# Seven block products for the query and output projections, and 2:4 comparisons summed in pairs

## The chip, the cores and the metric

The kernel runs on one core of one Trainium2 chip, in one launch. The metric is the device time in microseconds (us) of an execution, as the median over several runs; beside it stands one profiled execution, whose trace all views are read from. Engines are called as in the profile: PE (matrix multiplication), PEld (its weight loads), DVE (vector), ACT (scalar), POOL, and SP, whose queue issues all of the kernel's DMAs.

## The reference

Eight sequences of 512 tokens with 512 channels go through a "macaron" block, all in float32:

```
x = x + 0.5 * ffn(layernorm(x))        # FFN 1
x = x + attention(layernorm(x))        # 16 heads of 32 channels, 4 key/value heads
x = x + 0.5 * ffn(layernorm(x))        # FFN 2, same weights

ffn(x):        h = silu(x @ w_gate) * (x @ w_up)          # 2048 wide
               h = of each 4 neighbours keep the 2 largest in magnitude (ties: the first)
               return h @ w_down
attention(x):  Q = rope(x @ W_q); K = rope(x @ W_k); V = x @ W_v
               out = softmax(Q K^T / sqrt(32)) V           # K, V repeated over the heads
               return out @ W_o
```

`W_q` and `W_o` are 512 x 512; `W_k` and `W_v` are 512 x 128.

## The kernel before

**FFN.** There are 16 FFN passes (8 sequences, two each); each works through the hidden width in 4 pieces of 512 (`h`, indexed by `c`). The products of gate and up (`woven`, matmuls at L636) are not plain: each 512 x 512 product is cut into 2 x 2 blocks and made from seven block products instead of eight (a Strassen-Winograd scheme), with sums of blocks of the tokens (`ts`, made by `sums`) and sums of blocks of the weights (made once, in the first pass, by `combine_gu`, and kept in DRAM). The seven products go to three PSUM banks in the order x, v, x, v, x, z, x; between two products into a bank, DVE or ACT takes the bank's contents away (`copied`, L243 and L245, and `add`, L650), and the next product accumulates onto what is left in the bank. The down product (`products`, L561) is done the same way on blocks twice as deep; its weight sums are made by `combine_down` on POOL, its token-side sums `e` by POOL at L452 to L455.

**2:4 choice.** `keep_two_of_four` works on half of `h` at a time, [128, 4, 256]. ACT takes magnitudes (L407); DVE makes the six comparisons of the four neighbours as 0 or 1 in bf16 (L420 to L425), adds them up to four counts with eight operations on 128x256 elements (L429 to L441), and multiplies `h` by each count's comparison with a constant (L446). POOL's sums for the down product follow.

**Attention.** `attention(b)` runs as a "side": a generator whose steps are put between the products of the FFN passes of other sequences, so that PE always has FFN work between two steps. After its layernorm and transposes, `projected` makes K and then Q in four column blocks of 128, each with four matmuls 128x512 (L809) into one of three shared banks (`mm`); DVE rotates each block with four operations (shuffle of the bank, cosine times bank, sine times shuffle, add). V follows (L834). Then come, for each of four head groups, scores (L853) with maxima by DVE, transposed scores (L886, L891) with exponentials by ACT, the weighted sums (L902) and the division (L918 and after). Scores use a PSUM tile of four banks, `sc`. The output projection is four row blocks of 128 tokens with four matmuls 128x512 each (L988), and DVE adds each bank to the residual `xt` (L995), which goes to DRAM.

**What sets the order.** All instruction queues are written out in advance by a planner in the kernel: `at` holds its estimate of where PE, DVE and ACT stand; `multiplied` and `takes` advance it. DVE work that nobody needs at once is put in the queues `urgent` (`soon`), `put_off` (`later`) or `for_later`, and `fill`, called after each product, runs as much of it as is estimated to end with PE's queued work. `ensure` runs such work at once. A side has a first and a last place among the FFN products and a weight for each step (`WEIGHTS`); its next step is taken when it is due and its `ready` lies behind PE's place, or at the latest 3 groups (`LATE`) after it was due. One group is 3.45 us of PE time, as in L561's products of 16 records. PE, DVE, ACT, POOL and SP each run their own queue in order and meet through semaphores. Weight quarters of the FFN are prefetched 16 deep (`load_quarters`); `W_q`, `W_k`, `W_v` lie in one buffer of `wa_slots`, which `W_o` takes over.

Of the kernel before, what the change touches and what calls it, by code (L numbers as in the profile page):

```python
# [26 lines left out]
def macaron_block(  # L27
# [31 lines left out]
    wap = ctx.enter_context(tc.tile_pool(name="wap", bufs=1))  # L59
    qkvp = ctx.enter_context(tc.tile_pool(name="qkvp", bufs=1))  # L60
# [73 lines left out]
    identb = const.tile([P, P], BF, name="identb")  # L134

# [83 lines left out]
    wa_slots = Slots(wap, "wa", 1)  # L219
# [59 lines left out]
    def layernorm_t(got, tag, src=None, xb=None):  # L279
# [3 lines left out]
        xn = []  # L283
        for t in range(NT):
            xn.append(xnp.tile([P, D], FP, tag=tag, name="xn"))
            if xb is None:
                nc.sync.dma_start(out=xn[t], in_=src[t * P : (t + 1) * P, :])
# [39 lines left out]
        def sums():  # L327

            xT = got["xT"]
            (b11, b12), (b21, b22) = ([xT[:, 2 * i : 2 * i + 2, j * HALF : (j + 1) * HALF] for j in range(2)] for i in range(2))  # L330
            got["sums"] = ts = tp.tile([P, 4, 2, HALF], FP, tag="ts", name="ts")
            got["made"] = [
                later(0.62, partial(nc.vector.tensor_tensor, ts[:, i], a, b, ALU.subtract), at["act"])
                for i, a, b in ((0, b12, b11), (1, b22, ts[:, 0]), (2, b22, b12), (3, b21, ts[:, 1]))
            ]

        if xb is None:
# [21 lines left out]
            if tag == "xf":  # L359
                sums()  # L360
# [38 lines left out]
    def keep_two_of_four(h, made, sums=None, halves=(0, 1)):  # L399
# [14 lines left out]
        for half in halves:  # L414
            hh = h[:, :, half * HALF : (half + 1) * HALF]
            yield 0.7, at["act"] + HEARD

            m = sp.tile([P, 8, HALF], BF, tag="m", name="m")
            g01, g23, g02, g13, g03, g12, s0, s1 = (m[:, i, :] for i in range(8))
            nc.vector.tensor_tensor(m[:, 0:2, :], a[:, 0:4:2, :], a[:, 1:4:2, :], ALU.is_ge)  # L420
            yield 0.72, 0.0
            nc.vector.tensor_tensor(m[:, 2:4, :], a[:, 0:2, :], a[:, 2:4, :], ALU.is_ge)
            yield 0.7, 0.0
            nc.vector.tensor_tensor(g03, a[:, 0, :], a[:, 3, :], ALU.is_ge)
            nc.vector.tensor_tensor(g12, a[:, 1, :], a[:, 2, :], ALU.is_ge)  # L425
            taken = at["dve"]

            yield 0.4, 0.0
            nc.vector.tensor_tensor(s0, g01, g02, ALU.add)  # L429
            nc.vector.tensor_tensor(s1, g12, g13, ALU.add)  # L430
            yield 0.4, 0.0
            nc.vector.tensor_tensor(s0, s0, g03, ALU.add)
            nc.vector.tensor_tensor(s1, s1, g01, ALU.subtract)
            if half != halves[-1]:
                a = magnitudes(half + 1, taken + TOLD)
            yield 0.4, 0.0
            nc.vector.tensor_tensor(g02, g02, g12, ALU.add)
            nc.vector.tensor_tensor(g03, g03, g13, ALU.add)
            yield 0.4, 0.0
            nc.vector.tensor_tensor(g02, g23, g02, ALU.subtract)  # L440
            nc.vector.tensor_tensor(g03, g03, g23, ALU.add)  # L441
            for r, (s, op, n) in enumerate(
                ((s0, ALU.is_ge, 2.0), (s1, ALU.is_ge, 1.0), (g02, ALU.is_ge, 0.0), (g03, ALU.is_le, 1.0))
            ):
                yield 0.36, 0.0
                nc.vector.scalar_tensor_tensor(hh[:, r, :], s, n, hh[:, r, :], op, ALU.mult)  # L446
            if sums is not None:


                (h11, h21), (_, h22) = ([h[:, i::2, :HALF], h[:, i::2, HALF:]] for i in range(2))  # L450
                if half == 1:
                    nc.gpsimd.tensor_tensor(sums[:, 0], h21, h22, ALU.add)  # L452
                    nc.gpsimd.tensor_tensor(sums[:, 1], sums[:, 0], h11, ALU.subtract)
                    nc.gpsimd.tensor_tensor(sums[:, 2], h[:, 1::2, :HALF], sums[:, 1], ALU.subtract)
                    nc.gpsimd.tensor_tensor(h21, h11, h21, ALU.subtract)  # L455
            thin["halves"] = half + 1
# [39 lines left out]
    def combine_down(g):  # L496

        for c in range(2 * g, 2 * g + 2):
            raw = p_slots.tile([P, 4, D], FP, "raw")
            for r in range(4):  # L500
                nc.sync.dma_start(out=raw[:, r], in_=w_down[c][:, r])
                there = at["pe"] + 5.0
                yield now if r < 3 else lambda: there
            quarter = {f"{i + 1}{j + 1}": raw[:, i::2, j * HD2 : (j + 1) * HD2] for i in range(2) for j in range(2)}
            sums = wa_slots.tile([P, 6, 2, HD2], FP, "sums")

            for i, name in enumerate(SUMS):
                of = quarter[name[3:]] if name[3:] in quarter else sums[:, int(name[4:]) - 1]
                nc.gpsimd.tensor_tensor(sums[:, i], quarter[name[:2]], of, ALU.subtract)
                nc.sync.dma_start(out=combined[g, name][:, c % 2 * 2 : c % 2 * 2 + 2, :], in_=sums[:, i])  # L510
            yield now
# [270 lines left out]

    def attention(b):
        ensure(written[b, 0])
        wa = wa_slots.tile([P, ND, D + 2 * KV], FP, "wqkv")
        cs = p_slots.tile([P, 4, S], FP, "cs")
        loads = deque()
        for src, col in ((w_k, D), (w_v, D + KV)):
            loads.append((wa[:, :, col : col + KV], src.rearrange("(c p) n -> p c n", p=P)))
        for i in range(2):  # L790
            loads.append((cs[:, i], rope[i]))
        for k in range(ND):
            loads.append((wa[:, k, :D], w_q[k * P : (k + 1) * P, :]))
        got = {}
        for ready in layernorm_t(got, "xa", tokens[b][1]):
            if loads:
                dst, src = loads.popleft()
                nc.sync.dma_start(out=dst, in_=src)
# [6 lines left out]
        def projected(dst, col, scale):  # L805

            ps = Bank([P, S], "proj")
            for k in range(ND):
                nc.tensor.matmul(  # L809
                    out=ps.tile, lhsT=wa[:, k, col : col + P], rhs=xT[:, k, :], start=(k == 0), stop=(k == ND - 1)  # L810
                )
            multiplied(3.43)
            fill()
            sw = w_slots.tile([P, S], FP, "sw")
            soon(0.65, partial(nc.vector.stream_shuffle, sw, ps.tile, SWAP))
            read = soon(
                0.62, partial(nc.vector.scalar_tensor_tensor, dst, ps.tile, scale, cs[:, 0, :], ALU.mult, ALU.mult)
            )
            ps.free([read])
            soon(0.65, partial(nc.vector.scalar_tensor_tensor, sw, sw, scale, cs[:, 1, :], ALU.mult, ALU.mult))  # L820
            made = soon(0.65, partial(nc.vector.tensor_tensor, dst, dst, sw, ALU.add))
            return [p_slots.used(w_slots.used(made), 1)]

        of_k = projected(kT, D, 1.0)
        yield now
        of_q = []
        for c in range(ND):
            of_q.append(projected(qT[:, c, :], c * P, 1.0 / math.sqrt(HD)))
            yield now
        ensure(of_q[-1])  # L830
        vps = Bank([P, NT, KV], "vps")
        for t in range(NT):
            for k in range(ND):
# [3 lines left out]
                    rhs=wa[:, k, D + KV : D + 2 * KV],  # L837
# [7 lines left out]
        wo = wa_slots.tile([P, ND, D + 2 * KV], FP, "wo")  # L845
        yield partial(when, of_k + of_q[0])
# [88 lines left out]
        ensure(of_k + of_q[0])  # L935
        for t in range(NT):
            found = scores(0, t, nm)
            nc.sync.dma_start(out=wo[:, t, :D], in_=w_o[t * P : (t + 1) * P, :])
# [40 lines left out]
        xts = []  # L979
        for t in range(NT):  # L980
            xts.append(xnp.tile([P, D], FP, tag="xa", name="xt"))
            nc.sync.dma_start(out=xts[t], in_=tokens[b][1][t * P : (t + 1) * P, :])
        yield partial(when, out_of)
        waits(ensure(out_of))
        for t, xt in enumerate(xts):
            y = Bank([P, D], "y")
            for k in range(ND):
                nc.tensor.matmul(  # L988
                    out=y.tile, lhsT=qT[:, k, t * P : (t + 1) * P], rhs=wo[:, k, :D], start=(k == 0), stop=(k == ND - 1)
                )  # L990
            multiplied(3.43)
            fill()

            def add(t=t, xt=xt, y=y):
                nc.vector.tensor_tensor(xt, y.tile, xt, ALU.add)  # L995
                nc.sync.dma_start(out=tokens[b][2][t * P : (t + 1) * P, :], in_=xt)

            made = [soon(0.62, add)]
            y.free(made)
            if t == NT - 1:  # L1000
                ensure(made)
            yield now
# [8 lines left out]
    WEIGHTS = [0.5] * (NORM + ND + 2) + [0.7] * (NT + 1) + [0.9, 0.9] * NT  # L1011
    WEIGHTS += ([0.9, 1.2] + [0.9, 0.9] * (NT - 1)) * (ND - 2) + [1.5] + [1.3] * (NT - 1) + [1.5] + [0.5] * NT
# [6 lines left out]
    sides = [(10, 19, 10, partial(combine_down, 0), None, None), (22, 34, 10, partial(combine_down, 1), None, None)]  # L1019
# [109 lines left out]
```

## Time and profile before

| | us |
|---|---|
| median of 3 runs | 3211.94 |
| lowest, highest | 3211.62, 3216.32 |
| profiled execution, its own time | 3210.11 |
| its span, first to last instruction | 3208.2 |
| PE busy in it | 3176.9 |
| PEld busy | 2322.4 |
| DVE busy | 2189.8 |
| ACT busy | 1195.8 |
| POOL busy | 507.2 |

How to read it: the span is what the views cover; the profiled execution adds 1.9 us around it. A float32 matmul appears as two PE records. Records of neighbouring instructions overlap, since they are pipelined: what an instruction costs its engine is the distance from its start to the next one's start, which the chain and the timeline show, and not the record's own length. Idle time of an engine counts only if PE, whose work is nearly the whole span, ends up waiting for it.

### The profile page before, as it was taken

Reading aid. Unit: us, or ns where it says so; the run is one execution under the profiler, and the core shown is the slowest. Engines: PE = TensorE matmul, PEld = TensorE weight load, DVE = VectorE, ACT = ScalarE, POOL = GpSimd, SP = SyncE. Lnnn points to the kernel's source line nnn. Section 1 sums busy time; section 2 is a strip of 40 time slices with the busy share of each in tenths; the row PEclk is TensorE's granted clock in tenths of the full one; section 3 lists DMA queues with packets and bytes.
Section 4 is the critical chain, followed back from the end, with each engine's and each line's share of the span. In section 5 each row is a group of like instructions: output and inputs, shape, how many; then the busy total and the mean of one; then the engine's idle time right before and its main releaser. Section 6 shows DMA issues by size and latency. Waiting matters only on the chain.

```text
span 3208.2 us, 43276 instructions
## 1 busy us (share of the span) xinstructions
PE 3176.9 (99%) x15880; PEld 2322.4 (72%) x15880; DVE 2189.8 (68%) x4718; ACT 1195.8 (37%) x1683; POOL 507.2 (16%) x822
## 2 busy tenths in 40 slices
PE   8999999999999999999999999999999999999999
PEld 6887767767677677766776677766776677666886
DVE  7756876587657785678657865777567765776554
ACT  2222454145522553245314542255324441454220
POOL 2322102110021111101211102111120121111110
PEclk9999999999999999999999999999999999999999
DMA  7763344434443436334444344443633444434441
GB/s 236 240 216 99 122 158 144 142 128 126 156 158 126 132 119 210 96 121 152 145 143 131 122 153 159 133 132 112 210 99 119 161 141 142 131 122 154 154 165 53
DMA packets 263731, 462.15 MB, mean 144 GB/s; under 512 B 25952, under 2 KB 81760, under 8 KB 263264
## 3 DMA queue, kind: packets, MB, share of 16 engines
q1 hardware_dynamic: 263520, 459.38, 44.2%
q8 instruction: 127, 2.08, 0.3%
q14 instruction: 84, 0.69, 0.1%
HBM read 421.53 MB, written 37.75 MB: 143 GB/s over the span
## 4 chain that ended last, share of the span: by engine, by line
PE 96%; DVE 2%; DMA 1%; ACT 1%; POOL 0%; issue 0%; SPq 0%; POOLq 0%; DVEq 0%
PE x L636 27%; PE v L636 13%; PE x L561 13%; PE z L636 7%; PE v L561 6%; PE proj L809 4%; PE st L886 4%; PE sc L853 4%; PE ops L902 4%; PE y L988 3%; PE z L561 3%; PE tr L263 1%; PE gu L611 1%; PE den L918 1%; PE vps L834 1%; PE st L891 1%
## 5 line engine op out<-in xcount | busy, mean ns | idle before, releaser
L636 PE MATMUL x<-ts,w 128*128 128x256 f32 x3000 | 717.3, 382 | 1.4 <-DVE corner L650 1.4
L636 PEld LDWEIGHTS x<-ts,w 128*128 128x128 f32 x3000 | 561.7, 190 | 137.9 <-issue 44.3
L452 POOL TENSOR_TENSOR e<-h 128x512 f32<-128x512 f32 x62 | 79.3, 1279 | 2232.5 <-DVE h L446 1892.9
L165 DVE TENSOR_REDUCE nm<-sc 128x1 f32<-128x512 f32 x512 | 321.1, 683 | 95.3 <-PE sc L853 94.0
L561 PE MATMUL x<-wd,h 128*128 128x256 f32 x1488 | 339.9, 382 | 0.0
L165 DVE TENSOR_TENSOR total<-total,p 128x512 f32<-128x512 f32 x384 | 273.8, 749 | 81.1 <-ACT p L894 81.1
L561 PEld LDWEIGHTS x<-wd,h 128*128 128x128 f32 x1488 | 280.2, 190 | 62.5 <-issue 19.3
L894 ACT ACTIVATE p<-st 128x2048 f32<-128x2048 f32 x96 | 179.7, 1872 | 291.1 <-PE st L891 279.8
L255 ACT ACT_TABLE_LOAD x215 | 275.8, 1283 | 4.5 <-PEq L1118 0.7
L243 ACT COPY row<-x 128x512 f32<-128x512 f32 x207 | 121.2, 585 | 393.0 <-PE x L636 392.9
L685 ACT ACTIVATE h<-x 128x256 f32<-128x256 f32 x125 | 47.6, 381 | 555.2 <-PE x L636 543.3
L636 PE MATMUL v<-ts,w 128*128 128x256 f32 x1000 | 239.0, 382 | 2.4 <-ACT xT L324 2.4
L636 PE MATMUL x<-xT,w 128*128 128x256 f32 x1000 | 239.4, 382 | 1.8 <-ACT xT L324 1.8
L636 PE MATMUL v<-xT,w 128*128 128x256 f32 x1000 | 238.5, 382 | 1.5 <-DVE corner L245 1.5
L636 PE MATMUL z<-xT,w 128*128 128x256 f32 x1000 | 238.9, 382 | 0.0
L561 PE MATMUL v<-wd,e 128*128 128x256 f32 x992 | 228.2, 382 | 7.1 <-POOL e L452 4.0
L561 PEld LDWEIGHTS v<-wd,e 128*128 128x128 f32 x992 | 186.2, 190 | 52.6 <-issue 13.3
L636 PEld LDWEIGHTS x<-xT,w 128*128 128x128 f32 x1000 | 186.9, 190 | 49.2 <-issue 20.4
L636 PEld LDWEIGHTS v<-ts,w 128*128 128x128 f32 x1000 | 187.3, 190 | 46.2 <-issue 16.2
L636 PEld LDWEIGHTS z<-xT,w 128*128 128x128 f32 x1000 | 187.1, 190 | 45.6 <-issue 19.3
L636 PEld LDWEIGHTS v<-xT,w 128*128 128x128 f32 x1000 | 187.7, 190 | 42.8 <-issue 10.1
L407 ACT ACTIVATE a<-h 128x1024 f32<-128x1024 f32 x128 | 134.9, 1054 | 186.0 <-DVE m L425 106.8
(115 smaller groups left out, 4448.8 us busy)
## 6 DMA issues: line engine op xcount, KB each, us to landing
w<-gu SPq DMA_DIRECT2D x472, 256.0 KB, 3.4
w<-in_w_gu SPq DMA_DIRECT2D x394, 256.0 KB, 3.4
wd<-wd SPq DMA_DIRECT2D x124, 512.0 KB, 5.4
wd<-in_w_down SPq DMA_DIRECT2D x186, 256.0 KB, 3.6
x<-x SPq DMA_DIRECT2D x64, 256.0 KB, 2.6
xn<-x SPq DMA_DIRECT2D x64, 256.0 KB, 5.0
x<-in_x SPq DMA_DIRECT2D x32, 256.0 KB, 3.7
gu<-w SPq DMA_DIRECT2D x32, 256.0 KB, 2.9
```

Of the source, the lines that this page charges most:

```text
L165: self.does()
L243: nc.scalar.copy(dst, src)
L255: nc.scalar.activation(dummy[:, 1:2], dummy[:, 0:1], f)
L407: nc.scalar.activation(a, h[:, :, half * HALF : (half + 1) * HALF], AF.Abs)
L561: nc.tensor.matmul(out=y.tile[:, t, :], lhsT=part[:, t * P : (t + 1) * P], rhs=operands[i][:, n, :], start=(first and t == 0 and n == 0), ...
L636: nc.tensor.matmul(out=bank.tile[:, m, :], lhsT=lhs[:, m, k, :], rhs=rhs[:, k, :], start=(first and m == 0 and k == 0), stop=(k == 1), ski ...
L809: nc.tensor.matmul(out=ps.tile, lhsT=wa[:, k, col : col + P], rhs=xT[:, k, :], start=(k == 0), stop=(k == ND - 1))
L853: nc.tensor.matmul(out=sc[:, kv, :], lhsT=qT[rows, c, t * P : (t + 1) * P], rhs=kT[rows, :], start=True, stop=True)
L886: nc.tensor.matmul(out=st[:, kv, :], lhsT=kT[rows, t * P : (t + 1) * P], rhs=qT[rows, c, :], start=True, stop=False)
L894: nc.scalar.activation(p, st, AF.Exp)
L902: nc.tensor.matmul(out=ops[rows, :], lhsT=v[:, t, rows], rhs=p[:, kv, :], start=(t == 0), stop=(t == NT - 1))
L988: nc.tensor.matmul(out=y.tile, lhsT=qT[:, k, t * P : (t + 1) * P], rhs=wo[:, k, :D], start=(k == 0), stop=(k == ND - 1))
```

## The change

1. Q (without K) and the output projection are each made by seven block products, as in `woven`: blocks of 256 x 256, each product four matmuls 128x256, in the first three banks of the score tile `sc`, in the bank order 0, 1, 0, 1, 0, 2, 0. A product into a bank that was used before waits until DVE or ACT has taken what the bank held.
2. The sums of blocks of `W_q` and `W_o` are made once, by DVE, in the second FFN pass, and kept in DRAM. Weights then come one block (256 KB) at a time into a pool `waq` of 4 buffers, each loaded as one is used up.
3. The attention's tokens get sums of blocks too (`sums`, four DVE operations), and so do the heads' outputs (`combined_heads`, four more). The partial results are copied or added into `qT`, or added to the residual in place.
4. Scores begin when all of Q is rotated, not its first block alone. The rotation works on blocks of [128, 2, 256].
5. The table of cosines and sines is loaded once, not in each attention.
6. `combine_down` writes its sums in the four buffers of `waq`, not in one tile of `wa_slots`. The residual and the attention's layernorm input are one tile of four rows each, not four tiles.
7. In the 2:4 choice, five operations take the place of eight for the counts: three on two counts at once (128x512), one of which reads one comparison twice by a broadcast, and two on 128x256.
8. Steps and weights of the side follow.

```
@@ keep_two_of_four
-            nc.vector.tensor_tensor(s0, g01, g02, ALU.add)
-            nc.vector.tensor_tensor(s1, g12, g13, ALU.add)
-            nc.vector.tensor_tensor(s0, s0, g03, ALU.add)
-            nc.vector.tensor_tensor(s1, s1, g01, ALU.subtract)
...
-            nc.vector.tensor_tensor(g02, g02, g12, ALU.add)
-            nc.vector.tensor_tensor(g03, g03, g13, ALU.add)
-            nc.vector.tensor_tensor(g02, g23, g02, ALU.subtract)
-            nc.vector.tensor_tensor(g03, g03, g23, ALU.add)
+            g12, g03 = m[:, 5, :], m[:, 4:5, :].to_broadcast([P, 2, HALF])
+            g01_02, g13_23, g01_23, g02_13 = m[:, 0:2, :], m[:, 2:4, :], m[:, 0:4:3, :], m[:, 1:3, :]
...
+            s0_3 = m[:, 6:8, :]
+            nc.vector.tensor_tensor(s0_3, g01_23, g02_13, ALU.add)
+            nc.vector.tensor_tensor(g13_23, g13_23, g01_02, ALU.subtract)
...
+            nc.vector.tensor_tensor(s0_3, s0_3, g03, ALU.add)
+            s1, s2 = m[:, 2, :], m[:, 3, :]
+            nc.vector.tensor_tensor(s1, s1, g12, ALU.add)
+            nc.vector.tensor_tensor(s2, s2, g12, ALU.subtract)

@@ new: weights
+    def combine_qo():
+        for which, how in (("q", Q_SUMS), ("o", O_SUMS)):
+            both = [p_slots.tile([P, 4, 2, HALF], FP, "both") for _ in range(2)]
+            w = [both[q // 4][:, q % 4] for q in range(8)]
+            for q in range(4):
+                nc.sync.dma_start(out=w[q].rearrange("p a b -> p (a b)"), in_=flat(qo_raw[which][q]))
...
+            for to, a, b, op in how:
+                made = later(0.65, partial(nc.vector.tensor_tensor, w[to], w[a], w[b], op), queue=for_later)
+            yield partial(when, [made])
+            ensure([made])
+            nc.sync.dma_start(out=qo_sums[which], in_=both[1])
+            yield now

@@ attention: in place of projected() for Q
+        def seven(lhs, rhs, take):
+            sc = sc_slots.tile([P, N_KV, 2, HALF], FP, "seven")
+            waits(sc_slots.ready)
+            order = 0, 1, 0, 1, 0, 2, 0
+            taken = {bank: [] for bank in order}
+            for i, bank in enumerate(order):
+                waits(ensure(taken[bank]))
+                w = weights.popleft()
+                for m in range(2):
+                    for k in range(2):
+                        nc.tensor.matmul(out=sc[:, bank, m, :], lhsT=lhs(w, i, m, k), rhs=rhs(w, i, k), ...)
+                multiplied(1.73)
+                load_next()
+                fill()
+                taken[bank] = take(i, sc[:, bank])
...
+                yield partial(when, taken[order[i + 1]] if i < 6 else [])
...
+        def take_query(i, bank):
...
+            if i < 3:
+                return [Done(copied((left, corner, right)[i], bank))]
+            if i == 6:
+                return rotate(below, 0, bank)
+            to, j = ((right, 1), (corner, 1), (left, 0))[i - 3]
+            entry = soon(0.62, partial(nc.vector.tensor_tensor, to, bank, to, ALU.add))
+            rotate(to, j)
+            return [entry]
...
-        ensure(of_k + of_q[0])
+        ensure(of_k + of_q)

@@ attention: in place of the four row blocks of the output
+        made = [soon(0.62, partial(nc.vector.tensor_tensor, combined_heads[:, i], a, b_, op)) ...]   # 4 sums
+        def take_output(i, bank):
+            def add(to):
+                nc.vector.tensor_tensor(to, bank, to, ALU.add)
+                if i >= 5:
+                    for t in (0, 1) if i == 5 else (2, 3):
+                        nc.sync.dma_start(out=tokens[b][2][t * P : (t + 1) * P, :], in_=xt[:, t, :])
...

@@ the sides
-    WEIGHTS = [0.5] * (NORM + ND + 2) + ...  + [1.5] + [0.5] * NT
+    WEIGHTS = [0.5] * (NORM + 2 + 7 + 1) + ... + [1.5, 0.7] + [0.5] * 7
+    sides gets (36, 40, 2, load_cs, ...), (43, 56, 12, combine_qo, ...)
```

## The prediction

> **What bounds the kernel now.** I read the page's head first, then the chain that ended last.
>
> ```profile
> span 3208.2 us, 43276 instructions
> PE 3176.9 (99%) x15880; PEld 2322.4 (72%) x15880; DVE 2189.8 (68%) x4718; ACT 1195.8 (37%) x1683; POOL 507.2 (16%) x822
> PEclk9999999999999999999999999999999999999999
> PE 96%; DVE 2%; DMA 1%; ACT 1%; POOL 0%; issue 0%; SPq 0%; POOLq 0%; DVEq 0%
> ```
>
> PE's work is the span, at the full granted clock. The waits of PE alone say how little it lacks:
>
> ```profile
> PE tr L263 <- DVE xn L373: 7.4, 3, 6.4
> PE v L561 <- POOL e L452: 4.0, 4, 1.5
> PE st L886 <- DVE nm L165: 3.1, 2, 1.5
> PE v L561 <- DMA wd<-in_w_down: 2.9, 1, 2.9
> ...
> PE v L636 <- DVE corner L245: 1.5, 1, 1.5
> ...
> PE x L636 <- DVE corner L650: 1.4, 2, 1.2
> ```
>
> All of PE's waits together are some 27 us, 7.4 of them in the opening. So what this change is worth is decided by how many PE microseconds it removes, and by whether it gives PE something new to wait for. The rows of the matmuls concerned, by shape:
>
> ```profile
> L636 PE MATMUL x<-ts,w 128*128 128x256 f32 x3000 | 717.3, 382 | 1.4 <-DVE corner L650 1.4
> L636 PEld LDWEIGHTS x<-ts,w 128*128 128x128 f32 x3000 | 561.7, 190 | 137.9 <-issue 44.3 <-ACT corner L243 6.1 <-DVE row L650 4.0
> L809 PE MATMUL proj<-xT,wqkv 128*128 128x512 f32 x320 | 143.8, 592 | 0.0
> L988 PE MATMUL y<-wo,qT 128*128 128x512 f32 x256 | 115.1, 592 | 0.0
> L432 DVE TENSOR_TENSOR m<-m 128x256 bf16<-128x256 bf16 x128 | 37.2, 291 | 0.0
> ```
>
> The durations 382 and 592 ns overlap; prices are taken from the chain in order of time (start, us, what), in the first attention's projections:
>
> ```profile
> 245.31 1.73 PE x L636 x8
> 247.03 1.73 PE z L636 x8
> 248.76 3.43 PE proj L809 x8
> 252.19 1.73 PE x L636 x8
> 253.92 3.43 PE proj L809 x8
> 257.35 3.45 PE x L561 x16
> ```
>
> A block product (4 matmuls 128x256, 8 records) costs 1.73 us; a projection of one column block (4 matmuls 128x512, 8 records) 3.43. Changing from one kind to the other costs nothing. Between two steps of the side lies 1.73 to 3.45 us of FFN work on PE.
>
> **The change, part by part.**
>
> *PE work.* Q takes 4 x 3.43 = 13.72 us per attention now and 7 x 1.73 = 12.11 after: 1.61 less. With the finer distances (429 ns for 128x512, 215.7 for 128x256: 32 x 0.429 = 13.73 against 56 x 0.2157 = 12.08) it is 1.65. The output projection is the same again. 16 projections in 8 attentions: between 25.8 and 26.4, taken as **-26.2 us**. K, V, scores and FFN keep their matmuls; transposes too.
>
> [...] These weights fill all rows, and seven products need 56 loads where four blocks need 32. [...]
>
> *Waits between products.* Each seven has four re-uses of a bank (products 3, 4, 5 and 7), 64 in all. Uncovered, each would cost about 0.9 us (a DVE add of a bank is 0.69, and some 0.1 each for hearing of PE and for PE hearing of it): 58 us. The nearest row is L636 itself, which runs the same order of banks 125 times, with one product between a take and the next use, and waits for `corner` 2.9 us in all: 2.9 x 16 / 125 = 0.4 us. The side's products have FFN work between them besides, and are put off until their `ready`. I take **+0.5**. What is new beside L636 is that a taken bank may stand behind a rotation in the urgent queue; that is a rival below.
>
> *Scores wait for all of Q.* The last block comes with product 7: shuffle, cosine, sine, add, 0.60 to 0.71 us apart in the timeline, about 2.6 us, before the first score. Once per attention, 8 x 2.6 = 21 us if nothing covers it; the step is held back until the planner sees it ready and FFN products of 1.73 us go in its place. I take 0, with that upper end. K is ready long before.
>
> *DVE.* Per attention: 4 token sums, 3 adds and up to 3 copies for Q (ACT takes some, 0.585 each), 4 sums of heads and 3 more adds for the output: 14 to 17 operations of 0.69, 9.7 to 11.7 us, 77 to 94 in eight; rotations are as many as before. Once, 8 weight sums of 0.78 (the row of `w<-w`, L705): 6 us. The counts of the 2:4 choice cost 8 x 0.20 = 1.61 us per half now (start to start in the timeline; the records of 283 overlap). No row has a 128x512 bf16 addition. Its bounds are 0.20 and 0.60 us, the distance at 256 bf16 and at 512 f32 elements. [...] None of it is on PE's path; what hides it is DVE's idle 32%. That cover is thinnest in the projections: in 240 to 283 us DVE is busy 31.7 of 43, and gets 5 to 7 more. At 85 to 90% it still fits; a queue there shows as PE waits for `row` or `corner`, which I put at **+1.5** for all eight. The shorter counts might take back part of the 4.0 us of waits for `e`: -0.5, at most -4.
>
> *DMA and SP's queue.* Per attention, 4 loads of `W_q`, 4 of `W_o` and 2 of cosines become 14 blocks of 256 KB: 4 issues more (0.34 us each on SP) and 1 MB more, 8 MB on 462. SP waits for PE most of the time already (731 us for L636 alone), with 16 quarters, some 28 us of PE work, loaded ahead; a block load waiting for its buffer holds those behind it no longer than one product. A block lands in some 5 us (`wqkv` now); four are ahead, so at least three products and the FFN work between, 12 us or more. 0. The loads of `xn` for the next attention wait for the last store of `xt` (3.5 us) as the fourth does now: 0. The weight sums add 4 MB in the second pass, where DMA moves 99 to 122 GB/s against 240 before it, and the sums are due 2 groups before the first attention: 0, or up to 6 if DVE is forced through them at once. Three shared `mm` banks are freed from Q and output; PE waits for none there now: 0. POOL's sums for the down weights get the same four buffers in turns: 0.
>
> *Order.* The sides' steps fall on other places among the products, so that chance meetings, such as PE waiting about 1 us for a transposed block (at six places now), come and go: 0, by about 3 either way.
>
> Sum: -26.2 + 0.5 + 1.5 - 0.5 = **-24.7**. The profiled execution took 3210.11 (span and 1.9 around it), which is 1.8 under the median of the runs. 3210.1 - 24.7 = 3185.4, and 1.8 on top is 3187.2 for the median, 0.77% less: I say **3187**.
>
> **The rivals.**
>
> *A. Half the gain is lost in Q's phase.* A taken bank stands in the urgent queue behind a rotation: product 7 needs the add of product 5, which is behind the rotation of block 4, 2.6 us, and its own 0.6. If the planner lets it come late, PE waits 1 to 2 us per attention, and an FFN add behind it as long: about 12 us. 3199. For it: DVE at 85 to 90% there. Against: the same four operations stand in DVE's queue in the projections now, and no PE wait comes of them.
>
> *B. The same queue becomes the bound: slower.* The place is the stretch from product 4 of Q to the first score. A step that is not ready is forced 3 groups after it was due. If DVE is behind by more than that, PE stands for the rest of the rotations: up to 3.2 for product 7, then 2.6 for the last rotation, and again on FFN banks. It decides from 26.2 / 8 = 3.3 us per attention; with 5 us each it is -26 + 40, 3226. Against: 3 groups are 10 us, and DVE's queue would have to fall that far behind, with 15% of its time free.
>
> [...]
>
> **How the numbers follow.** Forecast 0.68 (own range 3180 to 3196), C with PE covered 0.06 (3190), A 0.10 (3193 to 3208), B 0.12 (over 3212), and 0.04 for something small that cancels all. Below 3180 is possible if the order also removes waits: hence 3178 as the low end. The high end goes up to 3208, into A; what is left out is B and a little below. A measurement of this kernel can tell about 0.2%, 6.4 us: faster is below 3205.5. That holds the forecast, C and most of A: 0.81. Same 0.07: the rest of A and the small one. Slower 0.12: B.
>
> **What would show it right or wrong.** No row of PE with 128x512 but K's and the last FFN's; a new row of 896 records, for Q and output together, 382 ns, starting 216 apart; PE busy about 26 us less, span about 25 less. PE's waits by these products and by scores under 5 us together; over 25 us there is B. [...] I am wrong if weight loads show between the new records, if the FFN's rows get idle time before them from DVE, or if steps of the side are forced before DVE is done with the bank.

## The result, and the profile after

The changed kernel takes 3194.55 us (median of 6 runs, 3193.66 to 3198.68), the kernel before 3214.89 in the same session (6 runs): a ratio of 0.994, 95% interval 0.9927 to 0.9953, faster by some 20 us. The forecast was 3187 in 3178 to 3208, and faster. Beside later experiments the changed kernel took 3194.47 against 3211.76, ratio 0.9944 (0.9932 to 0.9957).

The head of the page after, and its chain by engine:

```profile
span 3192.6 us, 43897 instructions
PE 3152.0 (99%) x16264; PEld 2391.1 (75%) x16264; DVE 2256.3 (71%) x4458; ACT 1176.2 (37%) x1663; POOL 525.6 (16%) x822
PE 92%; DVE 4%; DMA 2%; POOL 1%; ACT 1%; issue 0%; SPq 0%; DVEq 0%; POOLq 0%; ACTq 0%
```

PE is busy 24.9 us less, DVE 66.5 more, weight loads 69 more, and PE's share of the chain is down from 96% to 92%: PE waits more often. The span is only 15.6 shorter. (The profiled execution of before, 3210.11, lies 4.8 under the median of its six runs, that of after 0.1 under its own; so the two traces show 16 us of the 20.)

The new products, in two of their four groups by shape, and three of the counts of the 2:4 choice:

```profile
L889 PE MATMUL seven<-waq,sums 128*128 128x256 f32 x256 | 60.5, 379 | 0.0
L889 PEld LDWEIGHTS seven<-waq,sums 128*128 128x128 f32 x256 | 48.6, 190 | 6.6
L908 PE MATMUL proj<-xT,wkv 128*128 128x512 f32 x64 | 28.8, 592 | 0.0
L439 DVE TENSOR_TENSOR m<-m 128x512 bf16<-128x512 bf16 x128 | 55.6, 434 | 0.0
L441 DVE TENSOR_TENSOR m<-m 128x512 bf16<-128x512 bf16 x128 | 55.2, 431 | 3.3
L445 DVE TENSOR_TENSOR m<-m 128x512 bf16<-128x512 bf16 x128 | 54.5, 426 | 0.0
```

No PE idle time before the 896 records of L889, and hardly any for their weight loads. 128x512 is left to K in the projections. From each record's start to the next one's, Q and output took 219.9 us before (a wait of 0.8 behind them left out) and L889 takes 193.4: 26.5 saved.

What PE waits for, longest first (in total, times, longest):

```profile
PE v L569 <- POOL e L460: 11.5, 8, 2.0
PE tr L264 <- DVE xn L381: 7.6, 3, 6.5
PE v L569 <- DMA wd<-in_w_down: 3.2, 1, 3.2
PE st L1002 <- DVE nm L167: 3.1, 4, 1.8
PE vps L919 <- DVE kT L167: 2.4, 3, 0.8
```

Nothing waits in `seven`. But waits for `e`, the down product's sums that POOL makes after the 2:4 choice, went from 4.0 to 11.5 us, and V waits for K's bank, 2.4. All PE waits: 27.5 before, 36.7 after. And the granted clock is no longer full throughout. In these views (stretch, length, busy us of PE, PEld, DVE, ACT, POOL, then the clock) the stretches are cut at the steps of 3.41 us by which the clock changed in these traces, as the last section shows. Before:

```profile
103.41:106.83 3.42, 2.11 (x10) 1.52 (x8) 3.42 (x8) 1.00 (x1) 0.51 (x1) 1.00 0.87 308
106.83:110.24 3.41, 1.77 (x8) 1.39 (x9) 3.38 (x12) 0.06 (x1) 0.00 (x0) 1.00 1.01 358
```

and after

```profile
104.61:108.03 3.42, 0.18 (x2) 0.17 (x2) 3.38 (x11) 1.06 (x1) 0.00 (x0) 1.00 1.02 364
108.03:111.44 3.41, 3.41 (x9) 2.70 (x10) 2.44 (x6) 0.00 (x0) 1.01 (x2) 0.50 1.05 368
```

After PE's 3.2 us wait for `wd` the clock is at half for 3.4 us, which costs 1.7: the 16 records of L569 behind the wait take 5.38 us, and 3.62 at full clock. Before, the same wait (2.9) had no such sequel: it fell across two of these stretches and left PE idle for 1.3 and 1.6 us of them, where the 3.2 us lie in one. The balance of the two traces: -26.5 in the projections, +9.2 of waits and +1.7 of clock make -15.6, as in the span.

### The profile page after: what moved, and what is told of

The parts are those of the page before. It is cut to its first block, busy times and chain, and to the rows that moved or that the text cites. A ratio compares the mean times of both kernels' runs of the same rounds, so it can differ in the third digit from the quotient of the medians.

```text
span 3192.6 us, 43897 instructions
## 1 busy us (share of the span) xinstructions
PE 3152.0 (99%) x16264; PEld 2391.1 (75%) x16264; DVE 2256.3 (71%) x4458; ACT 1176.2 (37%) x1663; POOL 525.6 (16%) x822
## 4 chain that ended last, share of the span: by engine, by line
PE 92%; DVE 4%; DMA 2%; POOL 1%; ACT 1%; issue 0%; SPq 0%; DVEq 0%; POOLq 0%; ACTq 0%
PE x L644 25%; PE v L644 13%; PE x L569 13%; PE v L569 7%; PE z L644 6%; PE seven L889 6%; PE st L1002 4%; PE sc L969 4%; PE ops L1018 4%; PE z L569 3%; PE tr L264 1%; PE gu L619 1%; PE vps L919 1%; PE den L1034 1%; PE st L1007 1%; PE y L602 1%
## 5 line engine op out<-in xcount | busy, mean ns | idle before, releaser
L569 PE MATMUL x<-wd,h 128*128 128x256 f32 x1488 | 340.1, 382 | 0.8 <-DVE x L583 0.8
L569 PEld LDWEIGHTS x<-wd,h 128*128 128x128 f32 x1488 | 279.4, 190 | 61.6 <-issue 14.2
L569 PE MATMUL v<-wd,e 128*128 128x256 f32 x992 | 230.3, 384 | 14.8 <-POOL e L460 11.5
L569 PEld LDWEIGHTS v<-wd,e 128*128 128x128 f32 x992 | 187.2, 191 | 57.5 <-POOL e L460 14.7
```

Of the source, the lines that this page charges most:

```text
L569: nc.tensor.matmul(out=y.tile[:, t, :], lhsT=part[:, t * P : (t + 1) * P], rhs=operands[i][:, n, :], start=(first and t == 0 and n == 0), ...
```

## The experiments

### Which part brings the time: the 2:4 counts alone, seven alone, Q alone

`two_four_alone` is the kernel before with the five operations; `seven_alone` the changed one with the eight.

> The kernel before with the five-operation counts of the 2:4 choice alone. By the prediction DVE is busy some 10 us less (1.53 us per half by the starts in the trace, against 1.62) and the time is within 3 us of before, since PE does not wait for it; e waits between 1 and 5 us. If the planner's too low cost (0.34 counted for an operation that starts its successor 0.45 later) makes DVE late, e waits rise by 3 to 6 us, and the time with them.

> The changed kernel with the old eight-operation counts of the 2:4 choice. If the choice is off PE's path, the time is that of the changed kernel within 3 us (20 under before), with DVE busier by about 10 us. If the shorter counts were what kept e early, e waits grow from 11.5 by 0.1 to 0.2 per half in the tight places, 2 to 4 us more.

Counts alone: 3214.21 us against 3212.23, ratio 1.0004 (0.9995 to 1.0013): nothing. DVE is busy 2171.3 instead of 2189.8 (18.5 less, where 10 were expected), and PE's waits for `e` are 4.2. Seven alone: 3198.12, ratio 0.9955 (0.9942 to 0.9967), DVE 2278.9, waits for `e` 13.5 and for `nm` 8.9. So the gain comes with the products; under them the shorter counts may be worth some 4 us, but the intervals of 0.9955 and 0.994 overlap.

In `q_only` the output keeps its four blocks, with `W_o` by rows in the buffers of `waq`:

```
-        coming_qo = deque([("q", q) for q in SEVEN_Q] + [("o", q) for q in SEVEN_O])
+        coming_qo = deque([("q", q) for q in SEVEN_Q] + [("row", k) for k in range(ND)])
...
+                nc.tensor.matmul(out=y.tile, lhsT=qT[:, k, t * P : (t + 1) * P], rhs=wo[k], ...)   # for k, for t
```

> The changed kernel with the old output projection (four blocks of four matmuls 128x512, W_o by rows in the four buffers of waq). PE's work is 13.1 us over the changed kernel's; if the gain is PE work, the time is 8 to 13 us under before, and the row of the products in seven is 96.7 us long where the changed kernel's was 193.4. Waits for e are set by places, 6 to 9 us.

3203.97 us, ratio 0.9973 (0.9963 to 0.9984), 8.4 under before's 3212.4: half the products, about half the gain. The seven's starts span 96.8 us. The output's row is back:

```profile
L1108 PE MATMUL y<-waq,qT 128*128 128x512 f32 x256 | 115.1, 592 | 0.0
L892 PE MATMUL seven<-ts,waq 128*128 128x256 f32 x256 | 60.6, 380 | 0.0
```

Its waits for `e` are 8.4.

### Why PE waits more for e: less room, or other places

The changed side has 4 more steps before the scores and 4 more at the end, in the same length. From the first score to the last division's matmuls an attention has 213 to 225 us in the trace after, 233 to 239 before. First idea: the softmax's DVE work is squeezed, and the 2:4 choice is late. `before_squeezed` squeezes the kernel before by weights alone:

```
-    WEIGHTS = [0.5] * (NORM + ND + 2) + ...  + [1.5] + [0.5] * NT
+    WEIGHTS = [0.61] * (NORM + ND + 2) + ... + [1.5] + [1.03] * NT
```

> The kernel before, with no arithmetic changed: only the side's weights for layernorm, projections and output are raised (0.5 to 0.61, and 0.5 to 1.03 in the output), so that the stretch from the first score to the last division has as little room as in the changed kernel (some 220 us an attention in place of 236). Theory 'squeeze' (the same DVE work of the softmax in less time makes the 2:4 choice late, and PE waits for e): PE's waits for e go from 4.0 us to 8 to 14, and the time is 4 to 10 us over before. Theory 'more DVE work' (the sums, adds and copies that the change adds make DVE late): e waits stay at 4, the time within 3 us of before. Theory 'chance of places': e waits anywhere from 2 to 12.

3235.49 us, ratio 1.0065 (1.0051 to 1.0078): 23 us slower by weights alone. The stretch is 225 to 228 us, and PE's waits for `e` are 13.4 us, as the theory said:

```profile
PE v L561 <- POOL e L452: 13.4, 9, 2.0
```

The rest of the cost was not foreseen: other waits (for `xT`, `nm`, `wd`, `corner`) came up by 8.5 us, and the clock was at half for 17 us in four stretches, which is 8.5 more.

`after_pace` gives the changed kernel its room back:

```
-    WEIGHTS = [0.5] * (NORM + 2 + 7 + 1) + ...   + [1.5, 0.7] + [0.5] * 7
+    WEIGHTS = [0.413] * (NORM + 2 + 7 + 1) + ... + [1.5, 0.25] + [0.25] * 7
```

> The changed kernel, with the side's weights lowered where it has more steps (0.5 to 0.413 for the 23 first, 0.7 and 0.5 to 0.25 for the 8 last), so that the softmax stretch has its old room of about 236 us. Squeeze: waits for e fall from 11.5 to about 4, the time by 5 to 8 us against the changed kernel, 25 to 28 under before. More DVE work: e waits stay at 10 or more, same time as the changed kernel (20 under before). Rival A of the prediction: with 0.4 groups between products of the output there is less FFN work to cover a bank's taking, and waits for seven and kT come up by 3 to 10 us.

The theory fell: with 227 to 237 us of room, `e` waits are 14.4 us, not 4, and the time is 3204.67, ratio 0.9975 (0.9965 to 0.9985), 10 us over the changed kernel. Its PE waits:

```profile
PE v L569 <- POOL e L460: 14.4, 7, 5.9
PE tr L264 <- DVE xn L381: 7.5, 3, 6.4
PE tr L264 <- DVE row L658: 5.0, 2, 2.5
```

Both ways of moving the steps made waits. The timeline of one of them in the changed kernel shows what happens, first PE, then DVE and POOL (start, us, engine, line):

```profile
361.54 3.62 PE L569 MATMUL x<-wd,h 128*128 128x256 f32 x16
365.00 1.03 PE L569 MATMUL v<-wd,e 128*128 128x256 f32 x4
367.98 2.21 PE L569 MATMUL v<-wd,e 128*128 128x256 f32 x9 [1.96 <-POOL e L460]
```

```profile
360.62 0.68 DVE L167 TENSOR_TENSOR total<-total,p 128x512 f32<-128x512 f32 x1
361.22 0.42 DVE L454 SCALAR_TENSOR_TENSOR h<-m,h 128x256 f32<-128x256 bf16 x1
361.68 0.69 DVE L429 TENSOR_TENSOR m<-a 128x512 bf16<-128x512 f32 x1
...
365.09 1.43 DVE L454 SCALAR_TENSOR_TENSOR h<-m,h 128x256 f32<-128x256 bf16 x4
...
366.66 1.26 POOL L460 TENSOR_TENSOR e<-h 128x512 f32<-128x512 f32 x1 [67.90 <-DVE h L454]
```

The second half of a choice starts only as the last woven product ends, because softmax work (`total`, and the maxima `nm`) stood between the operations of the first half, which so took from 341.57 to 361.64 us. A half needs 5 us and POOL 1.3; one product of 3.45 lies between; the rest is PE's wait. Where softmax steps fall in relation to the end of a piece of `h` decides, and any change of weights shifts that. The planner does not count POOL, but from its clocks for DVE and PE, with POOL's 1.26 us added, these waits can be estimated before a run. Weights chosen so, with 2 to 3 us of them expected, are `after_weights`:

```
-    WEIGHTS = [0.5] * (NORM + 2 + 7 + 1) + ...  + [1.5, 0.7] + [0.5] * 7
+    WEIGHTS = [0.58] * (NORM + 2 + 7 + 1) + ... + [1.5, 0.7] + [0.45] * 7
```

> The changed kernel with other weights of the side alone: 0.58 for the 23 first steps (0.5), 0.45 for the last 7 (0.5); the softmax stretch gets even less room than in the changed kernel. Theory 'squeeze': waits for e rise above 11.5, and the time with them. Theory 'places' (a wait for e comes where softmax work stands in DVE's queue ahead of a 2:4 choice that is forced after the last woven product; reading the planner's own clocks, with POOL's 1.26 us added, this choice of weights leaves 2 to 3 us of them): e waits 2 to 5 us, the clock stays full, and the time is 6 to 9 us under the changed kernel, some 26 to 29 under before.

Waits for `e` are 2.7 us, in no more room (214 to 220 us in the second run's trace, 213 to 225 in the changed kernel's): place it is, not room. Nor is it the added DVE work as such, which is all still there (DVE busy 2263.8 us). The time, though, was 3192.22, ratio 0.9936 (0.9923 to 0.9948), and not 6 to 9 us better; nor did the clock stay full, with two stretches of 6.8 us at half in that profile. Both kernels again, side by side:

> The changed kernel once more, beside the next one on the same chip: 17 to 23 us under before, e waits 11.5, with one or two stretches of half clock after the longest waits of PE.

> The changed kernel with the side's weights 0.58 and 0.45, once more beside it: if placing e is worth what its waits say, 3 to 8 us under the changed kernel; if other waits take its place, as the first profile has them (den for mT 3.9, a longer half clock), within 3 us.

3194.47 (0.9944, 0.9932 to 0.9957) and 3191.24 (0.9937, 0.9924 to 0.9949): 3 us apart, with intervals that overlap. This is the best version found, clearly under the kernel before, and not told apart from the changed one. Its waits say where the `e` gain went:

```profile
PE tr L264 <- DVE xn L381: 7.5, 3, 6.4
PE den L1034 <- ACT mT L993: 3.9, 2, 2.5
PE v L569 <- DMA wd<-in_w_down: 2.9, 1, 2.9
PE v L569 <- POOL e L460: 2.7, 2, 1.3
```

`den` now meets an ACT copy, 3.9 us that the changed kernel doesn't have, and 1.3 more for `total`.

`after_choice_first` takes the softmax's additions out of the way altogether, by the order in `fill`: urgent, then steps of the choice, then put_off and for_later.

> The changed kernel with fill taking steps of the 2:4 choice ahead of put_off and for_later (rescaled totals, layernorm sums, and others): the softmax's additions no longer stand ahead of the choice. Places: waits for e go to about 1.5 (the first one, in the opening), but the additions are late in turn, and other waits (total, nm, seven) come up by about 10 us on the planner's clocks: the time is within 4 us of the changed kernel. More DVE work as such: e waits stay above 6.

3219.56 us, ratio 1.0022 (1.0013 to 1.0031), 25 over the changed kernel; I had said within 4. No wait for `e` is left in the list, but everything that was behind is late:

```profile
PE v L574 <- DMA wd<-in_w_down: 10.9, 1, 10.9
PE tr L264 <- DVE xn L381: 7.3, 3, 6.3
PE den L1039 <- ACT mT L998: 6.3, 4, 2.3
PE vps L924 <- DVE kT L167: 5.2, 3, 1.7
PE x L649 <- DVE corner L663: 4.9, 3, 2.3
```

The largest is in the opening pass. There SP, whose queue runs in order, stores DVE's sums of weights (`w`, in for_later) between its loads: from 60 to 120 us it waits 17.5 us for them, 10.9 in the changed kernel, and two loads of `wd` behind them go out at 112.0 us, not at 101.3. Waits are 50.3 us in all, and the clock is at half for 27.3 us (13.7 after that long wait).

### What hides the waits between products

In `burst` the seven products of a projection are one step, with no FFN product between (the `yield` in the loop of `seven` is gone; seven empty steps follow it).

> The changed kernel with the seven products of a projection in one step, with no FFN product between them: the cover that the prediction's +0.5 rests on is gone, and only the product into the other bank is left, as in the woven products of the FFN. If that alone is cover enough for a take (0.9 us against 1.73), PE waits for seven stay under 3 us in all. Rival A and B of the prediction: product 7 of Q waits for an add that stands behind a rotation, 1 to 3 us in each attention, 8 to 24 us in all. Besides, blocks 5 to 7 are loaded only when products 1 to 3 are done and land in about 5 us: up to 2 us per projection, 0 to 30 us. Time 10 to 40 us over the changed kernel if these are paid.

3295.97 us, ratio 1.0256 (1.0242 to 1.027): 101 us over the changed kernel, far over what I expected.

```profile
PE seven L889 <- DVE xt L1122: 31.9, 40, 1.3
PE seven L889 <- DVE qT L167: 18.3, 16, 1.4
PE seven L889 <- ACT qT L244: 16.2, 24, 0.7
```

80 waits, five in each projection, 66 us. A wait shows only from the end of the record before it; from start to start the seven take 281.1 us, 87.7 more than in the changed kernel, or 1.1 for each wait. Other waits came up by 8.9 us, and two more stretches of half clock cost 3.4. In the timeline of one, products 1 and 2, the latter in another bank:

```profile
252.38 1.89 PE L889 MATMUL seven<-xT,waq 128*128 128x256 f32 x8
254.31 0.58 ACT L244 COPY qT<-seven 128x512 f32<-128x512 f32 x1 [2.87 <-PE seven L889]
254.95 1.99 PE L889 MATMUL seven<-ts,waq 128*128 128x256 f32 x8 [0.67 <-ACT qT L244]
```

Product 2 waits for the copy of product 1, though bank 1 was free. The `seven` scheme counts on banks; what the program waits for looked like the tile. `burst_own_tiles` puts the two alternating banks in two tiles:

```
-            waits(sc_slots.ready)
-            order = 0, 1, 0, 1, 0, 2, 0
+            other = acc_slots.tile([P, 2, HALF], FP, "other")
+            waits(max(sc_slots.ready, acc_slots.ready))
+            bank_of = sc[:, 0], other
+            order = 0, 1, 0, 1, 0, 1, 0
```

> The burst, with its two alternating banks in two tiles of their own: bank 0 in the score tile, bank 1 in the tile of the weighted sums, which is free then, in the order 0, 1, 0, 1, 0, 1, 0. In the burst each product waited for the take of the product just before it, though that lay in another bank of the same tile, 80 times for 66 us in all. If this is because both banks lie in one tile, which is ordered as one, the waits of seven fall to under 25 us (what is left is takes behind rotations and blocks that are not loaded yet) and the time falls by 40 to 70 us against the burst. If the banks or DVE's and ACT's speed are what holds it, the waits stay at 60 or more.

3217.35 us, ratio 1.0016 (1.0007 to 1.0025), 79 under the burst; waits of the seven fall from 66 us to 8:

```profile
PE seven L891 <- DVE qT L167: 6.6, 8, 0.8
PE seven L891 <- DVE xt L1124: 1.3, 1, 1.3
```

So each product waits for the take just before it because both are of one tile. (Of the 23 us that remain over the changed kernel, 10 are in the seven by their starts and 10 in other waits.) The 6.6 that remain are once per attention, of takes behind a rotation: rival A's wait, at 0.8 us.

## Why the prediction was right, and where it was off

- **PE's work**, -26.2: 26.5 measured. This is the mechanism, and halving it (`q_only`) about halves the gain. Weight loads stayed beside the matmuls: the records of L889 start 216 ns apart with a load of 190 for each, as those of L636 did before, and 56 loads in place of 32 brought no PE idle time.
- **Waits between products**, +0.5: none in the changed kernel. But the ground was wrong, and the number held for another reason than the one given. I took L636 as the nearest row, where one product between a take and the next use is cover enough. There the banks are tiles of their own; here they are one tile, and a product waits for the take before it, whichever bank. What makes it nothing is the FFN work between steps alone, worth some 100 us by the burst; uncovered it is five waits of 1.1 us in each projection, not four of 0.9 (in the burst's timeline a copy takes 0.58; it starts 0.04 after PE's end, and PE 0.06 after it, not 0.1 each).
- **Scores wait for all of Q**, 0: right; no wait of `sc` is in the list.
- **DVE**: 2256 us. Without the counts it grows by 89 (2278.9 with the old counts, against 2189.8), within the 83 to 100 of the predicted additions, in part by luck: the operations added are 79 of it, with all 24 copies on ACT. The counts alone save 18.5: of the three on 128x512 two start the next 0.34 us later, the broadcast among them, and the first, L439, 0.45, all between the bounds of 0.20 and 0.60. L441 writes rows that L439 reads and waits for its semaphore, and starts 0.45 after it in 95 of the 96 places where it comes next; in four places an operation without that wait came next, 0.34 later, in others 0.45 or more: that the wait makes the difference was not shown.
- **A queue in the projections**, +1.5: V's 2.4 us wait for K's bank is the nearest to it: the four new token sums stand in DVE's queue ahead of K's rotation. Rivals A and B did not show.
- **The waits for e**, -0.5: this is the term that was mis-sized, +7.5 measured. No run shows the -0.5: with the shorter counts alone these waits went from 4.0 us to 4.2. I looked at them for the shorter counts only, and set what the new steps do to all places at 0 by about 3. The kernel before had weights under which softmax work and choices met seldom; in the trials here where weights or steps moved without regard to that, waits for `e` were 8 to 16 us.
- **The clock**: not in the sum. 1.7 us in the profile after.

-24.7 with these put in is -24.7 - 0.3 - 0.5 + 8.0 + 0.9 + 1.7, and -0.7 for all other waits: -15.6, the difference of the spans (3208.2 and 3192.6).

That 3194.55 lies in the range owes something to its width: the high end was put at 3208 for rival A, which did not come. Of the 9.1 us by which the traces fall short of -24.7, 8.0 are waits for `e`, which the prediction took to fall by half a microsecond.

## What to carry to other kernels

Where one engine is the whole span, count its instructions at their start-to-start distance: that number came out within 2% here. Then look for what the change does to the order of everything else. In a schedule written out ahead, a few more steps move every meeting of two engines, and a tuned set of places is lost with them: list the waits by releaser before and after, since they name those places.

## What the runs showed of the hardware

PE's waits can cost more than their length. Over the 13 profiles, after the opening, the granted clock went to half at or just after 18 of the 21 waits of PE of 2.2 us or more, 9 of the 40 of 1.7 to 2.2, and 1 of the 101 of 1.2 to 1.7; mostly for 3.4 us, up to four times that. `after_pace`, for one, after a wait of 1.8 us that ended at 2141.8 (the third number from the end is the clock's mean):

```profile
2141.00:2148.00 7.00, 6.18 (x27) 4.43 (x28) 5.54 (x15) 1.92 (x2) 1.50 (x4) 0.76 0.21 75
```

What tells the waits with such a sequel from the others in these traces is less their length than the idle time that they leave in a stretch of 3.41 us. In every profile the stretches of full and half clock, from the first full clock to the last change, are whole multiples of 3.41 us (27 for the 92.2 us before the half clock of the changed kernel, 4 for the longest half). Cut at that step from the first full clock on, the 13 profiles have 12073 stretches at full clock with PE idle for less than 1.66 us, and none of them was followed by one at half; of the 19 with 1.66 to 1.92 us of idle time 5 were, of the 23 with more all were. In the kernel before the most was 1.64 us, since its wait of 2.9 fell across two of them; in the changed kernel 3.24 had a sequel, and 1.80, at 1097.89, had none. Where the steps lie differs from profile to profile: the first full clock comes at 15.6 to 18.3 us (18.1 before, 15.9 after).

A stretch of 3.41 us at half clock costs 1.7, half of it by estimate (1.76 by the records of L569 above), so a wait of 2.2 us with a sequel costs nearly 4: 17 us at half clock account for 8.5 of the 28 us by which `before_squeezed` has the longer span.

That every product of the burst waited for the take of another bank of its tile, the other thing not expected, belongs to the program and not to the banks: the products wait for semaphores, and with the two banks in two tiles 71 of the 80 waits were gone.
